# A graph-attention kernel: seven of eight key-tile pairs added before their row sums, six sum tiles, sums three steps behind

## The chip, the cores and the metric

The kernel runs on one NeuronCore of a Trainium2 chip. The metric is device time in microseconds, the median of three runs: 4205.73 us for the kernel before (4204.49 to 4206.44). Engines are named as the profile names them: PE is the matrix engine (PEld its weight load), DVE the vector engine, ACT the scalar engine, POOL the GpSimd engine, SP the engine that issues most DMAs.

## The reference, cut to what matters

Eight batches of 2048 nodes with 256 features go through two attention layers with four heads each, over one adjacency matrix. The change touches the second layer only:

```python
def _L1_gnn_ref(h, adj, W, a):
    ...
    q = (h @ W).reshape(B, N, H, D)
    a_src, a_dst = (a[:D], a[D:])
    e_src = jnp.einsum('bnhd,d->bnh', q, a_src)
    e_dst = jnp.einsum('bnhd,d->bnh', q, a_dst)
    e = e_src[:, :, None, :] + e_dst[:, None, :, :]
    e = jnp.where(e >= 0, e, ALPHA * e)
    mask = (adj > 0)[None, :, :, None]
    e = jnp.where(mask, e, NEG_INF)
    attn = jax.nn.softmax(e, axis=2)
    h_prime = jnp.einsum('bijh,bjhd->bihd', attn, q)
    return jax.nn.elu(h_prime.reshape(B, N, H * D))
```

The softmax needs two things for each node i: the weighted sum over the nodes j, and the plain sum of the weights over j, which divides it.

## The kernel before, in words

The first layer's loop (lines 748 to 788) is untouched. The second layer is one loop over 512 rounds (lines 901 to 952): 32 passes k (one batch and head each, `passes`), each of 16 steps jt, one for each tile of 128 key nodes j. The weights of a tile stand as 128 keys by 2048 queries, in four blocks of 512.

In a step, these things are issued:

- DVE makes the tile of weights e (`clipped`, L804) from near, which lies in PSUM and is written once a pass by ACT (`nears`, L795), from a number of its own for each key (far), and from the mask (limit). It does so two steps ahead of the rest (`ready`). There are five e tiles (`second_e`). At steps 0 and 15 the operation is split into two halves.
- PE multiplies the tile with the values (`weigh_rows`, L815), eight calls into two PSUM banks (acc).
- The sum over the keys is made on PE as well (`add_up_rows`, L826), four calls of the tile against for_sums into one PSUM bank (den). To spare such calls, two neighbouring tiles 2m and 2m+1, the pair m, are first brought together in t: at the even step ACT scales the first tile by the ratio of the two keys' factors into t (L926, two halves), at the odd step POOL adds the second tile to t (L932, two halves), and PE sums t LAG = 2 steps later, from the list `due`. Pairs 3 and 7 (`SINGLE`) are not added: PE sums each of their tiles unadded, in the step in which it comes. t has four buffers of 128 x 1024, so two pairs; they use memory (tag q) that the first layer needed for its queries.
- At step 15 ACT copies acc (cT, L939), PE makes the sums that are due, and ACT copies den (dT, L948). The pass's `ending` (lines 838 to 878) is then a generator that later steps carry on: PE transposes dT and cT, DVE makes the inverse and z (L848, L858), ACT four small operations for each half (L870 to L873), POOL two adds for each half (L875, L876), SP stores. Step 0 of the next pass begins with ACT's for_sums (L911).

`advance()`, at the end of every step but 13, moves such generators on: the ending, and during heads 0 to 2 the `preparation` of the next batch (normalised rows h, transposed hT, the values qn on PE and DVE, small work on POOL). Each engine carries out what it was given strictly in the order of issue, which is the order of this loop: a schedule written out by hand.

In the first passes the first layer's last block is still being finished (`finish`, L517 and L553 on POOL, tile o with two buffers); its last store of o falls into pass 1.

Of the kernel before, what the change touches and what calls it, by code (L numbers as in the profile page):

```python
# [27 lines left out]
def bcast(ap, axis, n):  # L28

    ap = ap.unsqueeze(axis)  # L30
    shape = list(ap.shape)
    shape[axis] = n
    return ap.broadcast_to(shape)
# [18 lines left out]
def layers(  # L52
# [24 lines left out]
    NQB = N // QB  # L77
    NKT = N // P
# [20 lines left out]
    def banks(name):  # L99
        return [psum.tile([P, QB], F32, tag=f"both{k}", name=name) for k in range(2)]  # L100
# [5 lines left out]
    def heads_tile(name, tag, bufs=2):  # L106
        return big.tile([P, 2, QB], F32, tag=tag, name=name, bufs=bufs)
# [105 lines left out]
    def advance(all_of=True, mask_first=False):  # L213

        moved = all_of and tick()
        for steps_of in sorted(aside, key=lambda steps_of: mask_first and steps_of is not all_limits):
            got = next(steps_of, aside)
            if got is aside:
                aside.remove(steps_of)
            moved = moved or got is not False  # L220
            if got is None:
                if here[0] < 0:
                    aside.append(aside.pop(aside.index(steps_of)))
                break
        return moved

    def drain(until=lambda: False):
        while not until() and advance():
            pass
# [359 lines left out]
    def sources(held, h, **place):  # L589

        es = []
        for half in range(2):
            e = big.tile([P, HALF], F32, name="es", **place)
            nc.sync.dma_start(
                e,
                held[h, 2 * half : 2 * half + 2, :, :]
                .rearrange("b c p -> (b c p)")
                .partition_broadcast(P),
            )
            es.append(e)  # L600
        return es
# [208 lines left out]
    def weigh_rows(jt, h, e, qn, acc):  # L810

        for part in range(2):
            own = slice(h * DH + 32 * part, h * DH + 32 * part + 32)
            for blk in range(NQB):
                nc.tensor.matmul(  # L815
                    acc[part][32 * blk : 32 * blk + 32, :],
                    qn[jt // NT][:, jt % NT, own],
                    e[:, blk, :],
                    start=(jt == 0),
                    stop=(jt == NKT - 1),  # L820
                )

    def add_up_rows(jt, blocks, for_sums, den, first, last):

        for blk in range(NQB):
            nc.tensor.matmul(  # L826
                den[32 * blk : 32 * blk + 32, :],
                for_sums[:, jt, :],
                blocks[blk],
                start=first,  # L830
                stop=last,
            )
# [44 lines left out]
            yield True  # L877
        nc.sync.dma_start(column(out[b], h), xs)

    LAG = 2  # L880
    SINGLE = (3, NKT // 2 - 1)
    first_layer.close()
    second_e = ctx.enter_context(tc.tile_pool(name="second_e", bufs=5))
    psum = ctx.enter_context(tc.tile_pool(name="second_psum", bufs=1, space=PSUM))
# [6 lines left out]
    def begun(k, jt):  # L891

        b, h = passes[k]
        if jt == 0:
            nears(near, following.pop(k), h, shared[b][2])
        return clipped(jt, h, near, shared[b][3], jt in (0, NKT - 1))
# [3 lines left out]
    due, ts, acc, den, before = [], None, None, None, None  # L900
    for s, (k, jt) in enumerate(rounds):
        here[0] = len(steps) + s // 4
        b, h = passes[k]
        qn, held, off_s, far, quot, share = shared[b]
        if s + 2 < len(rounds):
            ready.append(begun(*rounds[s + 2]))
        now = ready.pop(0)
        if jt == 0:
            acc = banks("acc1")
            for_sums = big.tile([P, NKT, 32], F32, tag="sr"[k % 2], name="for_sums", bufs=1)  # L910
            nc.scalar.copy(for_sums, bcast(share[:, :, h], 2, 32))  # L911
            if h == 0 and b + 1 < B:
                aside.append(preparation(b + 1))
        if jt == (2 if k % 4 < 3 else 8) and k + 1 < len(passes):
            b1, h1 = passes[k + 1]
            drain(lambda: b1 in shared)
            following[k + 1] = sources(shared[b1][1], h1, tag="add")
        weigh_rows(jt, h, now, qn, acc)
        m = jt // 2
        if m in SINGLE:  # L920
            due.append((s, jt, [now[:, blk, :] for blk in range(NQB)]))
        elif jt % 2 == 0:
            ts = []
            for half in range(2):
                t = heads_tile("t", "q", 4)
                nc.scalar.activation(  # L926
                    t, now[:, 2 * half : 2 * half + 2, :], AF.Copy, scale=quot[:, m, h : h + 1]
                )
                ts.append(t)
        else:  # L930
            for half in range(2):
                nc.gpsimd.tensor_tensor(  # L932
                    ts[half], ts[half], now[:, 2 * half : 2 * half + 2, :], ALU.add
                )
            due.append((s + LAG, jt, [ts[blk // 2][:, blk % 2, :] for blk in range(NQB)]))
        if jt == NKT - 1:
            cT = big.tile([P, 2, QB], F32, tag="hT", name="cT", bufs=1)
            for part in range(2):
                nc.scalar.copy(cT[:, part, :], acc[part])  # L939
        for entry in [entry for entry in due if entry[0] <= s]:  # L940
            due.remove(entry)
            _, j, blocks = entry
            if j == 1:
                den = rest[0][:, 0, :]
            add_up_rows(j, blocks, for_sums, den, j == 1, j == NKT - 1)
        if jt == NKT - 1:
            dT = const.tile([P, QB], F32, tag="wk", name="dT")
            nc.scalar.copy(dT, den)  # L948
            aside.insert(0, ending(k, cT, dT))

        if jt != NKT - 3:
            advance()
# [252 lines left out]
@with_exitstack  # L1205
def adj_preln_kernel(
    ctx: ExitStack,
    tc: tile.TileContext,
    x, adj, Wq, bq, Wk, bk, Wv, bv, Wo, bo, gamma, beta, W, a, out,
):  # L1210
    nc = tc.nc
    B, N, F = x.shape
    const = ctx.enter_context(tc.tile_pool(name="const", bufs=1))
    dram = ctx.enter_context(tc.tile_pool(name="dram", bufs=1, space=bass.MemoryType.DRAM))
    ident = const.tile([P, P], F32, tag="ident", name="ident")
    make_identity(nc, ident)
    x1 = [dram.tile([N, F], F32, tag=f"x1_{b}", name=f"x1_{b}") for b in range(B)]
    verdict = const.tile([1, 1], I32, tag="verdict", name="verdict")
    layers(
        tc, x, adj, Wq, bq, Wk, bk, Wv, bv, Wo, bo, gamma, beta, W, a, x1, out, ident, dram, verdict  # L1220
    )
    with tc.If(nc.values_load(verdict, min_val=0, max_val=1) != 0):  # L1222
        gat_layer(tc, x1, adj, W, a, out, ident)
# [35 lines left out]
```

## Time and profile before

| | us |
|---|---|
| median of three runs | 4205.73 |
| the profiled execution | 4210.55 |
| its span, first to last instruction | 4208.7 |
| second layer, first e tile to the last dT | 2729.1 to 4191.2 |
| mean granted clock of PE | 0.994 |

The profile comes from one execution. The page gives, for each engine, the busy time over the span; the windows view gives the same for a stretch; the timeline lists instructions in order, with the start, the duration (of several merged ones, if it says x2 or more: PE's matmuls count two records for a call), and in brackets the idle time of the engine before it and what ended it. The busiest groups of the second layer, from the page:

| line, engine | what | count | busy us | mean ns |
|---|---|---|---|---|
| L804 DVE | e (both widths) | 576 | 1183.0 | 2107 |
| L815 PE | acc | 8192 | 972.8 | 595 |
| L932 POOL | t + e | 384 | 903.9 | 2383 |
| L926 ACT | t from e | 384 | 420.1 | 1144 |
| L826 PE | sums of t | 1536 | 211.0 | 594 |
| L826 PE | sums of e | 1024 | 141.0 | 592 |

PE's records overlap, since several matmuls run side by side, so their mean is not the time that PE gives to one of them; the distance of their starts in the timeline is.

### The profile page before, as it was taken

The numbers are of one execution on the slowest core, as the hardware profiler recorded it, in microseconds if no ns is written. First come the engines' busy times: TensorE is split into PE (matmuls) and PEld (weight loads), VectorE is DVE, ScalarE is ACT, GpSimd is POOL, SyncE is SP. The second block draws the span as 40 slices with busy tenths as digits, with TensorE's granted clock in tenths as the row PEclk, the third lists the DMA queues.
The fourth block names the chain that finished last, engine by engine and source line by source line (L and its number), as shares of the span: only waits on it lengthen the run. The fifth ranks groups of instructions, "written<-read, shape, count | busy, mean of one in ns | idle before, by whom it ended". The sixth has DMA issues, their size and how long they took to land. (4 is left out here: it accounts for less than half of the span.)

```text
span 4208.7 us, 85702 instructions
## 1 busy us (share of the span) xinstructions
PE 4067.2 (97%) x34998; PEld 1507.0 (36%) x34998; DVE 3159.1 (75%) x3526; ACT 2394.9 (57%) x3090; POOL 3263.0 (78%) x1735
## 2 busy tenths in 40 slices
PE   7999999999999999999999999889999999999998
PEld 3333333333333333333333333333333333333333
DVE  5786676666766677676677677588888988888897
ACT  5655565555565565555556556564555646555554
POOL 2577787888888888788788799777776877777687
PEclk9999999999999999999999999999999999999999
DMA  3221211112112112111211222221221222122121
GB/s 112 87 77 50 57 58 48 53 53 65 48 55 63 48 51 61 54 50 53 62 50 54 55 60 62 80 58 51 63 71 33 72 52 73 51 63 71 33 61 37
DMA packets 343235, 248.11 MB, mean 59 GB/s; under 512 B 225840, under 2 KB 293168, under 8 KB 342832
## 3 DMA queue, kind: packets, MB, share of 16 engines
q1 hardware_dynamic: 337648, 223.66, 19.6%
q0 software_dynamic: 5184, 18.88, 1.2%
q8 instruction: 277, 4.54, 0.4%
q14 instruction: 126, 1.03, 0.1%
HBM read 204.15 MB, written 36.18 MB: 57 GB/s over the span
## 5 line engine op out<-in xcount | busy, mean ns | idle before, releaser
L449 DVE SCALAR_TENSOR_TENSOR E<-big,limit 128x1024 f32<-128x1024 f32 x1024 | 1181.9, 1217 | 646.1 <-PE big L441 627.9
L742 POOL TENSOR_TENSOR add<-E 128x1024 f32<-128x1024 f32 x512 | 1203.7, 2374 | 496.1 <-PE both L461 472.7
L455 ACT ACTIVATE E<-E 128x1024 f32<-128x1024 f32 x1024 | 1055.7, 1057 | 687.8 <-DVE E L449 669.1
L804 DVE SCALAR_TENSOR_TENSOR e<-near,far,limit 128x2048 f32<-128x2048 f32 (+1 forms) x576 | 1183.0, 2107 | 94.3 <-issue 55.0
L932 POOL TENSOR_TENSOR t<-t,e 128x1024 f32<-128x1024 f32 x384 | 903.9, 2383 | 346.4 <-ACT t L926 196.0
L461 PE MATMUL both<-E,v 128*32 128x512 f32 x8192 | 993.9, 594 | 0.2
L815 PE MATMUL acc<-e,qn 128*32 128x512 f32 x8192 | 972.8, 595 | 5.3 <-DVE e L804 5.1
L441 PE MATMUL big<-qT,kT 64*128 64x512 f32 x4096 | 959.4, 606 | 14.6 <-DVE E L449 12.5
L441 PEld LDWEIGHTS big<-qT,kT 64*128 64x128 f32 x4096 | 366.2, 187 | 587.7 <-issue 419.8
L926 ACT ACTIVATE t<-e,quot 128x1024 f32<-128x1024 f32 x384 | 420.1, 1144 | 266.5 <-DVE e L804 153.1
L501 POOL TENSOR_TENSOR acc<-acc,c 128x1024 f32<-128x1024 f32 x224 | 531.2, 2371 | 4.6 <-DVE c L499 4.6
L461 PEld LDWEIGHTS both<-E,v 128*32 128x32 f32 x8192 | 294.3, 109 | 535.8 <-issue 396.7
L815 PEld LDWEIGHTS acc<-e,qn 128*32 128x32 f32 x8192 | 271.8, 110 | 496.0 <-issue 451.4
L499 DVE TENSOR_TENSOR c<-both,r 128x512 f32<-128x512 f32 x448 | 308.7, 690 | 42.3 <-PE both L461 10.6
L472 PE MATMUL big<-add,ones 128*32 128x512 f32 x2048 | 280.7, 601 | 13.9 <-POOL add L742 3.4
L826 PE MATMUL rest<-t,for_sums 128*32 128x512 f32 x1536 | 211.0, 594 | 22.2 <-DVE z L858 9.5
L479 ACT COPY s<-big 128x512 f32<-128x512 f32 x256 | 149.8, 585 | 71.1 <-PE big L472 70.8
L826 PE MATMUL rest<-e,for_sums 128*32 128x512 f32 x1024 | 141.0, 592 | 0.0
L145 ACT ACTIVATE h<-x,off,rstd 128x256 f32<-128x256 f32 x256 | 139.2, 593 | 0.0
L154 PE MATMUL rest<-w,hT 128*32 128x256 f32 x1952 | 122.1, 392 | 10.7 <-DVE qn L693 6.6
L795 ACT ACTIVATE near<-es,off_s 128x1024 f32<-128x1024 f32 x64 | 71.6, 1119 | 106.8 <-DVE e L804 95.8
L154 PE MATMUL big<-hT,wk 128*32 128x512 f32 x1024 | 124.2, 600 | 7.0 <-ACT hT L165 5.8
(133 smaller groups left out, 3031.3 us busy)
## 6 DMA issues: line engine op xcount, KB each, us to landing
r<-inv SPq DMA_DIRECT2D x1024, 64.0 KB
x<-in_x_dram SPq DMA_DIRECT2D x96, 512.0 KB
es<-er SPq DMA_DIRECT2D x64, 512.0 KB
adj_in<-in_adj_dram SPq DMA_DIRECT2D x32, 512.0 KB
x<-o POOLq DMA_DIRECT2D x32, 512.0 KB, 3.3
xh<-x SPq DMA_DIRECT2D x32, 512.0 KB
out_dram<-xh SPq DMA_DIRECT2D x32, 512.0 KB
x<-x SPq DMA_DIRECT2D x28, 512.0 KB
```

What stands on the lines that cost most here:

```text
L441: nc.tensor.matmul(ps[:, hh, :], ks[kt // NT][own, hp, (kt % NT) * P : (kt % NT + 1) * P], qs[qb][own, hp, :], start=True, stop=True,)
L449: nc.vector.scalar_tensor_tensor(e, ps, -0.5, bcast(limit[:, qb, kt, :], 1, 2), ALU.max, ALU.min)
L455: nc.scalar.activation(e, e, AF.Exp, scale=0.25 * EDGE)
L461: nc.tensor.matmul(both[part][32 * h : 32 * h + 32, :], vs[kt // NT][:, kt % NT, mine], es[h // 2][:, h % 2, :], start=first, stop=not first,)
L499: nc.vector.tensor_tensor(to[:, part, :], both[part], r, ALU.mult)
L501: nc.gpsimd.tensor_tensor(acc, acc, to, ALU.add)
L742: nc.gpsimd.tensor_tensor(both, tiles[0][hp], tiles[1][hp], ALU.add)
L804: nc.vector.scalar_tensor_tensor(e[:, of, :], near[:, of, :], far[:, jt, h : h + 1], limit[:, of, jt, :], ALU.max, ALU.min,)
L815: nc.tensor.matmul(acc[part][32 * blk : 32 * blk + 32, :], qn[jt // NT][:, jt % NT, own], e[:, blk, :], start=(jt == 0), stop=(jt == NKT - 1),
L826: nc.tensor.matmul(den[32 * blk : 32 * blk + 32, :], for_sums[:, jt, :], blocks[blk], start=first, stop=last,)
L926: nc.scalar.activation(t, now[:, 2 * half : 2 * half + 2, :], AF.Copy, scale=quot[:, m, h : h + 1])
L932: nc.gpsimd.tensor_tensor(ts[half], ts[half], now[:, 2 * half : 2 * half + 2, :], ALU.add)
```

## The change

Pair 3 is added like the others; only pair 7 is still summed tile by tile. The sums come three steps after the addition instead of two, but never later than step 15. t gets two more buffers: from pass 3 on, pairs 2 and 5 use the two buffers of o, which the first layer has left; in passes 0 to 2 all pairs share the four of tag q.

```diff
-    LAG = 2
-    SINGLE = (3, NKT // 2 - 1)
+    LAG = 3
+    SINGLE = NKT // 2 - 1
...
-        if m in SINGLE:
+        if m == SINGLE:
             due.append((s, jt, [now[:, blk, :] for blk in range(NQB)]))
         elif jt % 2 == 0:
             ts = []
             for half in range(2):
-                t = heads_tile("t", "q", 4)
+                t = heads_tile("t", "o", 2) if k > 2 and m % 3 == 2 else heads_tile("t", "q", 4)
...
-            due.append((s + LAG, jt, [ts[blk // 2][:, blk % 2, :] for blk in range(NQB)]))
+            due.append((min(s + LAG, s - jt + NKT - 1), jt, [ts[blk // 2][:, blk % 2, :] for blk in range(NQB)]))
```

## The prediction

> **What bounds the kernel now.** The page first: which engine is full, over the whole span.
>
> ```profile
> PE 4067.2 (97%) x34998; PEld 1507.0 (36%) x34998; DVE 3159.1 (75%) x3526; ACT 2394.9 (57%) x3090; POOL 3263.0 (78%) x1735
> ```
>
> The change touches only the second layer, whose 32 passes (one head of one batch each) run from 2729 us to the end. A pass ends when dT (L948), its finished column of sums, is copied. I read the times of those copies from the timeline of ACT and cut the windows view there. From batch 1 to 6 the pass lengths repeat within 0.1 us, so four rows of batch 3 (heads 0 to 3) and one of the last batch stand for nearly all. The columns are window, length, then busy time of PE, weight load, DVE, ACT and POOL.
>
> ```profile
> core 0: us, PE busy (x) PEld busy (x) DVE busy (x) ACT busy (x) POOL busy (x), PEclk, DMA share, GB/s
> 3294.90:3341.50 46.60, 44.01 (x396) 14.35 (x392) 41.68 (x25) 29.16 (x42) 36.95 (x20) 1.00 0.34 103
> 3341.50:3384.30 42.80, 42.11 (x400) 14.57 (x404) 36.62 (x24) 27.14 (x38) 33.26 (x16) 1.00 0.23 54
> 3384.30:3437.20 52.90, 51.54 (x576) 19.19 (x568) 44.91 (x34) 22.67 (x31) 33.83 (x19) 1.00 0.10 22
> 3437.20:3478.50 41.30, 40.37 (x382) 14.88 (x384) 36.29 (x23) 21.90 (x26) 33.33 (x16) 1.00 0.25 69
> 4069.90:4110.30 40.40, 39.08 (x350) 13.94 (x348) 37.97 (x23) 21.86 (x27) 33.29 (x16) 1.00 0.21 59
> ```
>
> PE is idle 0.7 to 2.6 us a pass: it sets the pace in heads 1 to 3. In the last batch DVE is just as full: 37.97 us plus the 2.39 us in which it waits for ACT's near (L795) make the 40.4. POOL has 7 to 10 us free (19 in head 2), so the question is where that free time lies. The timelines of PE, ACT and POOL at the turn into a last-batch pass, and through it:
>
> ```profile
> 4067.87 1.07 PE L826 MATMUL rest<-t,for_sums 128*32 128x512 f32 x8
> 4068.73 1.07 PE L826 MATMUL rest<-e,for_sums 128*32 128x512 f32 x8
> 4069.59 2.48 PE L815 MATMUL acc<-e,qn 128*32 128x512 f32 x16
> ```
>
> ```profile
> 4069.86 0.58 ACT L948 COPY dT<-rest 128x512 f32<-128x512 f32 x1 [1.13 <-PE rest L826]
> 4070.34 0.62 ACT L911 COPY for_sums<-share 128x512 f32<-128x512 f32 x1
> 4070.86 2.20 ACT L926 ACTIVATE t<-e,quot 128x1024 f32<-128x1024 f32 x2
> ```
>
> ```profile
> 4072.53 4.71 POOL L932 TENSOR_TENSOR t<-t,e 128x1024 f32<-128x1024 f32 x2 [6.30 <-DVE e L804]
> 4077.42 4.70 POOL L932 TENSOR_TENSOR t<-t,e 128x1024 f32<-128x1024 f32 x2 [0.17 <-DVE e L804]
> 4082.63 1.29 POOL L875 TENSOR_TENSOR z<-z,low 128x512 f32<-128x512 f32 x1 [0.51 <-ACT z L872]
> 4083.99 1.29 POOL L876 TENSOR_TENSOR xh<-xh,z 128x512 f32<-128x512 f32 x1
> 4085.24 4.73 POOL L932 TENSOR_TENSOR t<-t,e 128x1024 f32<-128x1024 f32 x2
> 4089.93 1.29 POOL L875 TENSOR_TENSOR z<-z,low 128x512 f32<-128x512 f32 x1
> 4091.30 1.29 POOL L876 TENSOR_TENSOR xh<-xh,z 128x512 f32<-128x512 f32 x1
> 4092.54 14.12 POOL L932 TENSOR_TENSOR t<-t,e 128x1024 f32<-128x1024 f32 x6
> ```
>
> POOL's free time is one piece, 6.30 us before a pass's first pair; after it POOL runs almost without a gap to the last add of pair 6 (4106.66). PE sums that pair at step 15, sums the unadded pair 7, ACT copies dT, then builds for_sums, then the first t, and only then can POOL add again. Today DVE's second e tile (4072.36) comes 0.4 us later than t, so the loop is nearly closed, but not the bound.
>
> **The change, part by part.**
>
> *Removed:* for pair 3, two sums of e (steps 6 and 7) become one sum of t. A sum is 4 calls (8 records) and holds PE 4068.73 - 4067.87 = 0.86 us: 0.86 a pass, 27.5 us over 32.
>
> *Added on ACT:* two scalings L926, 2.20 us a pair. ACT is idle 17 to 30 us a pass: nothing. They stand at step 6, where ACT's next work (z of the second half, hT copies) is not late; if it were, at most 2.2 us a pass.
>
> *Added on POOL:* two adds L932. In 4092.54 to 4106.66 three pairs follow each other at (14.12 - 4.73)/2 = 4.69 us. POOL's order of issue puts pair 3 after the second z/xh and right before pair 4. Pairs 4 to 6 are already back to back there, so all of it is pushed on, less whatever gap stood in front of pair 4.
>
> *Sums a step later, six t buffers:* a pair is summed at step +3 instead of +2, but the min() keeps pair 6 at step 15, as now. Where sums came too early (PE's weight loads waited 41.8 us for POOL's t in 51 waits) the later step helps; the third pair of t buffers takes ACT's 113.3 us of waiting for L826 away, which POOL's work will outlast. In passes 0 to 2 t keeps four buffers with the later sums; POOL has 20 us free in 0 and 2. I take nothing for these. No DMA is added, removed or moved past another on SP's or POOL's queue.
>
> *The wait this makes:* PE's sum of pair 6 must wait for POOL. Behind it in PE's queue stand the sum of pair 7 and the next pass; behind that ACT's dT, for_sums and t; behind those POOL itself. A pass is then three terms: a, from dT to POOL's first add; r, POOL's run to the end of pair 6; c, from there to the next dT. Closed, c is 4069.86 - 4067.87 = 1.99 plus a hop of 0.1 = 2.09 (now 2.6 to 4.5, because PE comes later than POOL). And a is 0.48 + 0.52 on ACT to the start of t, 1.14 for its first half and a hop of 0.1: 2.24, which the trace shows in head 3 (3437.22 to 3439.46).
>
> - Last batch: now 2.67 + 34.13 + 3.64 = 40.44. After: r gains 4.69 and loses the 0.51 wait for z (POOL now gets there later): 2.24 + 38.31 + 2.09 = 42.64, **+2.20**.
> - Head 3: now 2.24 + 35.48 + 3.61. After 2.24 + 40.17 + 2.09 = 44.50, **+3.17**. Its waits of 1.50 and 0.50 us (DVE's e behind the last qn, z) come after dT too and stay.
> - Head 1: now 4.55 + 35.39 + 2.83. POOL waits 1.98 us before pair 4, which pair 3 fills: 4.55 + 38.10 + 2.09 = 44.74, **+1.97**. Its long a holds the hT copy and two h that ACT has in its queue there.
> - Head 0: now 2.67 + 39.47 + 4.46. A gap of 1.70 is filled: 2.24 + 42.46 + 2.09 = 46.79, **+0.19**.
> - Head 2: POOL has gaps of 2.82 and 2.90 us before pairs 5 and 6 and is done 8 us before PE asks. PE keeps the pace: -0.86, and because PE now starts 1.5 us later against DVE, about half of its 1.2 us of waits for the inverse and z goes too: **-1.5**.
>
> Batches 1 to 6: 6 x (0.19 + 1.97 - 1.5 + 3.17) = +23.0. Batch 0: pass 0 is PE's (-0.9); pass 1, where POOL also finishes the first layer's last block and is busy 39.2 of 45.2 us, 3.17 + 39.47 + 4.69 + 2.09 = 49.4 against 45.25 (+4.1); pass 2 -1.5; pass 3, 2.24 + 38.60 + 2.09 = 42.93 against 39.78 (+3.15): +4.9 in all. Last batch: 4 x 2.20 = +8.8; what follows the last dT is as before. Sum **+36.7 us**: the span goes from 4208.7 to about 4245 us. The profiled execution took 4210.55, 4.8 above the median of 4205.73; the difference is put on the median: **4242 us**.
>
> *The e buffers.* Five e tiles, and POOL now also holds tile 7 until pair 3 is added. DVE's step 12 needs tile 7, step 14 needs tile 9. In a last-batch pass POOL would free tile 9 some 1 us after DVE wants it even if the loop above did not exist: DVE alone would make a pass about 41.6, +1.2. It lies inside the loop's +2.2, and costs on top only if DVE's delay reaches the next pass's second e, up to 1 us a pass.
>
> *Where the Trainium skill weighs.* By "Perfetto Trace Analysis", section "Optimizing Scalar/DVE Operations", GpSimd and VectorE share a read port of SBUF, so moving work between them may not help. If each added add stopped DVE for its length, that were 32 x 4.7 = 150 us more. The rows say otherwise: L804's 2048-wide form takes 2342 ns where POOL is idle and 2344 where POOL adds throughout (largest 2353), and L932 stays within 2346 to 2422. I take 0. By the same page's "Identifying the Most-Contended Engine", PE's matmul time is no good measure and POOL's occupancy is, which makes POOL (78%) the engine to relieve. By the page's reading the PE cut is worth 0; by the rows above, where PE idles 0.7 us in 42.8, it is worth 0.86 wherever POOL is not asked for more, which leaves head 2.
>
> **Rivals.**
>
> 1. *POOL's free 6.3 us swallow the pair, and PE's saving is kept* (faster). PE is short of time in 28 passes: 28 x 0.86 = 24 us less, 4182. For it: POOL is idle more than 4.69 us in every pass. Against: the gap lies behind the deadline. Pair 6 is ready only 1.65 us before PE asks in the last batch (0.86 in head 1, 1.64 in head 3, 2.5 in head 0); this is faster only where filled gaps plus that lead exceed 4.69 + 0.86, true in head 2 alone.
> 2. *Only DVE's e buffers bind, the loop hides* (little slower): +1.2 in heads 3 and last, 0 in heads 0 and 1, -1.5 in head 2: 11 x 1.2 - 7 x 1.5 + 4 = +7, about 4212. It needs a and c to overlap with POOL's run; ACT's and PE's orders of issue speak against it.
> 3. *The loop plus lost cover* (slower still): PE's sums of pairs 3 to 5 also stall, and DVE's late tiles push the next pass: +1 us in some 25 passes, about 4267.
> 4. *The change does not do what it says:* PE's order of issue shows 128 calls fewer and pair 3 among the sums of t. Under 1%.
>
> **How the numbers follow.** The loop 0.66 (4225 to 4260), rival 1 0.11, rival 2 0.12, rival 3 0.10, change without effect 0.01. Within 0.2% (about what a measurement of this kernel can tell from no change) is 4197 to 4214: half of rival 2 and the last, 0.06. Faster 0.11, slower 0.83. The range 4218 to 4262 holds the loop, the upper part of rival 2 and half of rival 3; its low end is heads 1 and 3 gaining 1 us each back.
>
> **What would show it.** Right: passes of 42.6 in the last batch, 44.5 in heads 1 and 3, 46.8 in head 0, 51.4 in head 2; POOL's free piece shrunk to 4.3 us and ended by ACT's t, not by DVE's e; PE's sum of pair 6 starting 0.1 us after POOL's last add, PE idle 3 us before it; L804 and L932 at unchanged lengths. Wrong: PE reaching the sum of pair 6 after POOL (rival 1), POOL's first add still released by DVE (rival 2), L804 longer beside POOL (the port).

## The result, and the profile after

The changed kernel takes 4233.72 us (median of five runs; the kernel before took 4204.49 in the same job): 1.0070 times as long, 95% interval 1.0054 to 1.0086. That is +29.2 us; forecast were +36.7 and 4242 us. One of the five ran at a granted clock of 0.579, took 6665.06 us, and is left out of the ratio. The profiled execution took 4233.72, its span is 4231.9. First the page, then the windows view cut at the dT copies, for the same five passes as before (batch 3, heads 0 to 3, and one of the last batch); columns as above.

```profile
PE 4078.6 (96%) x34742; PEld 1495.5 (35%) x34742; DVE 3162.0 (75%) x3526; ACT 2463.1 (58%) x3154; POOL 3412.2 (81%) x1799
```

```profile
core 0: us, PE busy (x) PEld busy (x) DVE busy (x) ACT busy (x) POOL busy (x), PEclk, DMA share, GB/s
3302.60:3348.80 46.20, 43.78 (x385) 14.16 (x376) 38.26 (x23) 31.45 (x44) 41.49 (x22) 1.00 0.31 89
3348.80:3393.40 44.60, 42.83 (x396) 15.77 (x400) 39.58 (x25) 29.25 (x40) 37.88 (x18) 1.00 0.24 53
3393.40:3444.00 50.60, 50.37 (x564) 18.83 (x556) 43.62 (x34) 24.66 (x34) 38.48 (x21) 1.00 0.10 23
3444.00:3488.30 44.30, 42.30 (x380) 14.07 (x384) 38.44 (x24) 24.03 (x28) 37.97 (x18) 1.00 0.28 76
4088.00:4130.30 42.30, 40.29 (x344) 12.94 (x340) 38.21 (x23) 23.94 (x28) 37.89 (x18) 1.00 0.19 52
```

POOL has 4.6 us more in every pass. Heads 1 and 3 and the last batch are longer, head 2 is 2.4 us shorter and now PE's alone (50.37 of 50.60). In head 3 and the last batch neither PE nor DVE is full any more (last batch: PE 40.29, DVE 38.21 of 42.30). The timelines of PE, ACT and POOL at the turn of a pass in the last batch show why:

```profile
4086.07 0.62 PE L826 MATMUL rest<-t,for_sums 128*32 128x512 f32 x2 [0.75 <-POOL t L932]
```

```profile
4088.03 0.59 ACT L948 COPY dT<-rest 128x512 f32<-128x512 f32 x1 [2.36 <-PE rest L826]
4088.51 0.62 ACT L911 COPY for_sums<-share 128x512 f32<-128x512 f32 x1
4089.03 4.28 ACT L926 ACTIVATE t<-e,quot 128x1024 f32<-128x1024 f32 x4
```

```profile
4083.65 2.37 POOL L932 TENSOR_TENSOR t<-t,e 128x1024 f32<-128x1024 f32 x1
4090.26 9.43 POOL L932 TENSOR_TENSOR t<-t,e 128x1024 f32<-128x1024 f32 x4 [4.24 <-ACT t L926]
...
4109.58 18.74 POOL L932 TENSOR_TENSOR t<-t,e 128x1024 f32<-128x1024 f32 x8
4132.56 2.39 POOL L932 TENSOR_TENSOR t<-t,e 128x1024 f32<-128x1024 f32 x1 [4.24 <-ACT t L926]
```

Read in order of time it is one ring. POOL's last add of pair 6 ends at 4086.02; PE's sum of its second half starts 0.05 us later; dT follows at 4088.03, for_sums, t, and POOL adds again at 4090.26, released by ACT's t where DVE's e released it before. POOL's free piece is 4.24 us (it was 6.30), and each of its two ends is now set by POOL itself. The next free piece begins 4.24 us before 4132.56: a period of 42.30.

Pass lengths below are distances of the dT copies. The first layer is not touched, and its end moves between 2722.3 and 2729.1 us from profile to profile, so I compare the sum of the 32 passes instead of spans. Heads are medians of batches 1 to 6.

| kernel | head 0 | head 1 | head 2 | head 3 | last batch | 32 passes against before | median, us |
|---|---|---|---|---|---|---|---|
| before | 46.62 | 42.77 | 52.91 | 41.33 | 40.44 | 0 | 4204.5 |
| changed | 46.23 | 44.61 | 50.55 | 44.35 | 42.27 | +29.5 | 4233.7 |
| no adds of pair 3 | 44.64 | 42.76 | 50.59 | 41.51 | 40.43 | -22.6 | 4182.9 |
| half of the adds of pair 3 | 44.12 | 42.74 | 50.60 | 42.02 | 40.43 | -16.8 | 4186.0 |
| deferred | 45.67 | 41.91 | 53.52 | 40.08 | 41.37 | +2.0 | 4207.2 |
| add only | 47.78 | 45.09 | 51.75 | 44.82 | 42.73 | +50.5 | 4255.9 |
| sums later, six buffers | 44.16 | 43.06 | 52.31 | 41.51 | 40.43 | -15.8 | 4188.5 |
| sums later only | 44.16 | 43.06 | 52.31 | 41.52 | 40.43 | -14.5 | 4190.4 |
| six buffers only | 46.62 | 42.77 | 52.91 | 41.34 | 40.43 | +0.1 | 4203.3 |
| pair 3 added in head 2 only | 44.16 | 43.06 | 51.45 | 41.52 | 40.43 | -18.9 | 4184.7 |

### The profile page after: what moved, and what is told of

Its sections match the earlier page's. It is cut to its first block, busy times and chain, and to the rows that moved or that the text cites. A ratio compares the mean times of both kernels' runs of the same rounds, so it can differ in the third digit from the quotient of the medians.

```text
span 4231.9 us, 85391 instructions
## 1 busy us (share of the span) xinstructions
PE 4078.6 (96%) x34742; PEld 1495.5 (35%) x34742; DVE 3162.0 (75%) x3526; ACT 2463.1 (58%) x3154; POOL 3412.2 (81%) x1799
## 5 line engine op out<-in xcount | busy, mean ns | idle before, releaser
L804 DVE SCALAR_TENSOR_TENSOR e<-near,far,limit 128x2048 f32<-128x2048 f32 (+1 forms) x576 | 1186.6, 2105 | 141.4 <-POOL t L932 118.0
L932 POOL TENSOR_TENSOR t<-t,e 128x1024 f32<-128x1024 f32 x448 | 1053.2, 2388 | 235.2 <-ACT t L926 205.5
L815 PE MATMUL acc<-e,qn 128*32 128x512 f32 x8192 | 1008.0, 596 | 8.7 <-DVE e L804 8.0
L926 ACT ACTIVATE t<-e,quot 128x1024 f32<-128x1024 f32 x448 | 488.3, 1142 | 197.1 <-DVE e L804 129.0
L826 PE MATMUL rest<-t,for_sums 128*32 128x512 f32 x1792 | 293.7, 595 | 33.1 <-POOL t L932 30.1
L826 PEld LDWEIGHTS rest<-t,for_sums 128*32 128x32 f32 x1792 | 67.2, 109 | 212.7 <-issue 113.1
```

The costliest lines, as they stand in the source:

```text
L804: nc.vector.scalar_tensor_tensor(e[:, of, :], near[:, of, :], far[:, jt, h : h + 1], limit[:, of, jt, :], ALU.max, ALU.min,)
L815: nc.tensor.matmul(acc[part][32 * blk : 32 * blk + 32, :], qn[jt // NT][:, jt % NT, own], e[:, blk, :], start=(jt == 0), stop=(jt == NKT - 1),
L826: nc.tensor.matmul(den[32 * blk : 32 * blk + 32, :], for_sums[:, jt, :], blocks[blk], start=first, stop=last,)
L926: nc.scalar.activation(t, now[:, 2 * half : 2 * half + 2, :], AF.Copy, scale=quot[:, m, h : h + 1])
L932: nc.gpsimd.tensor_tensor(ts[half], ts[half], now[:, 2 * half : 2 * half + 2, :], ALU.add)
```

## The experiments

The theory is the ring: POOL's adds, PE's sum of pair 6, dT, for_sums, t, POOL. Its rivals are a cost of POOL's adds by their sheer time (port, or an engine that is full), and a cost of the later sums. Ratios are to the kernel before in the same job: 4206.39 us for the runs without the adds, deferred, addition alone and rest alone, 4204.25 for the other four. Differences in us between runs of different jobs carry the 2 us by which the jobs differ. The diffs shown are against the changed kernel. The runs with none or half of pair 3's adds leave tile 7, or half of it, out of the row sums.

**Without the adds of pair 3.**

```diff
-            for half in range(2):
+            for half in range(2) if m != 3 else ():
                 nc.gpsimd.tensor_tensor(
```

> Pair 3 is scaled and summed as one tile, but POOL's two adds for it are left out, so tile 7 is missing from the row sums. Theory (the loop through POOL's 4.69 us of added work): POOL's run is back to six pairs, PE keeps its 0.86 us, so the passes of the last batch return to about 40.4 us, head 1 to about 41.9, head 3 to about 40.5, head 2 stays near 50.5: about 4180 us (4172 to 4190). Rival (the loss lies in the longer PE order, the later sums or the added ACT work, not in POOL's adds): it stays above 4220 us.

Measured: 4182.86 us, 0.9940 (0.9927 to 0.9954), as expected, though heads 1 and 3 took 0.9 and 1.0 us more than expected. By the sums of the passes, two POOL instructions a pass are worth 52 us over 32 passes, although POOL is idle 4.4 us a pass even with them in the last batch. The loss is theirs: ACT's scaling and the new order of PE's sums are still in this run.

**The sum of pair 6 and dT one step later.** The ring is cut in the order of issue; nothing of the work changes.

```diff
-            due.append((min(s + LAG, s - jt + NKT - 1), jt, [...]))
+            due.append((s + LAG, jt, [...], k, for_sums))
...
-            add_up_rows(j, blocks, for_sums, den, j == 1, j == NKT - 1)
-        if jt == NKT - 1:
-            dT = const.tile([P, QB], F32, tag="wk", name="dT")
-            nc.scalar.copy(dT, den)
-            aside.insert(0, ending(k, cT, dT))
+            add_up_rows(j, blocks, sums_of, den, j == 1, j == NKT - 3)
+            if j == NKT - 3:
+                column_done(of, cT, den)
...
```

(column_done holds the three lines taken out; after the last round the same is done for what is left in `due`.)

> All seven pairs are added as in the changed kernel, but the sum of pair 6 and the copy dT that follows it move to step 0 of the next pass (no min() any more), so the next pass's for_sums and t no longer stand behind them in ACT's queue. Theory (a closed loop POOL, PE's last sum, dT, for_sums, t, POOL): the loop opens, POOL's first add starts with DVE's second e again, and the next bounds are the five e tiles in the last batch and head 3 (about 41.6 us a pass) and PE elsewhere: about 4193 us (4185 to 4210). Rival (POOL simply has too much to do): no change, above 4225 us.

Measured: 4207.20 us, 1.0003 (0.9995 to 1.0012), inside the expected range but 14 us above its centre. With the same POOL work the passes lose 2.0 us instead of 29.5. ACT's and POOL's timelines at the turn (here L917 is for_sums, L932 ACT's t, L904 dT, L938 POOL's add):

```profile
4063.50 0.62 ACT L917 COPY for_sums<-share 128x512 f32<-128x512 f32 x1
4064.02 2.19 ACT L932 ACTIVATE t<-e,quot 128x1024 f32<-128x1024 f32 x2
4067.12 0.59 ACT L904 COPY dT<-rest 128x512 f32<-128x512 f32 x1 [0.90 <-PE rest L826]
```

```profile
4059.24 4.73 POOL L938 TENSOR_TENSOR t<-t,e 128x1024 f32<-128x1024 f32 x2
4066.67 9.39 POOL L938 TENSOR_TENSOR t<-t,e 128x1024 f32<-128x1024 f32 x4 [2.69 <-DVE e L804]
```

The t of the next pass now stands ahead of dT, and POOL is again released by DVE's e. A last-batch pass takes 41.37 us, not 40.44: DVE waits 0.85 us for POOL's hold on an e tile, which is the e-buffer bound (41.6 in the prediction):

```profile
4096.01 4.73 DVE L804 SCALAR_TENSOR_TENSOR e<-near,far,limit 128x2048 f32<-128x2048 f32 x3 [0.85 <-POOL t L938]
```

Passes 0 and 1 are 5 and 6 us longer than in the kernel before. Head 2 is 3.0 us longer than in the changed kernel, head 3 4.3 shorter. I did not trace either to its instruction.

**Half of the adds of pair 3.**

```diff
-            for half in range(2):
+            for half in range(1 if m == 3 else 2):
                 nc.gpsimd.tensor_tensor(
```

> As the changed kernel, but POOL adds only the first half of pair 3, so the row sums lack tile 7 for half of the queries. Theory (a loop through POOL that has to grow past the other bounds before it costs anything): 2.36 us less than the changed kernel brings the last batch from 42.3 back to DVE's 40.4, head 3 to about 42.0, head 1 to PE's and DVE's 42.8, head 0 to about 44.6: about 4188 us (4182 to 4197), nearly all of the way back to the kernel without the adds. Rival (POOL's adds cost by their sheer time, through a port or through the engine's total): half of the way, about 4208 us.

Measured: 4185.96 us, 0.9957 (0.9944 to 0.9971). With no add 4182.9, with one 4186.0, with two 4233.7: the first costs 3 us, the second 48. By the sums of the passes it is 5.8 and 46.3, and all of the 5.8 lies in batch 0; in batches 1 to 6 and the last the first half costs nothing. That is a ring growing past other bounds, not a price by the microsecond of POOL.

**The addition alone**, with sums two steps behind and four buffers (`LAG = 2`, all t of tag q).

> Pair 3 is added, but the sums stay two steps behind and t keeps four buffers. Theory: the loop is as closed as in the changed kernel, since pair 6 is summed at step 15 in both; on top of it t waits for the sums of four buffers: 4233 to 4255 us. Rival (the addition is harmless, the later sums cost): about 4205 us or less.

Measured: 4255.89 us, 1.0116 (1.0100 to 1.0131), 0.9 us above the theory's range and far from the rival's. So the rest of the change does not cost but gives: 22 us (21 by the sums of the passes).

**The rest of the change alone**, pairs 3 and 7 unadded.

```diff
-    SINGLE = NKT // 2 - 1
+    SINGLE = (3, NKT // 2 - 1)
...
-        if m == SINGLE:
+        if m in SINGLE:
```

> Pairs 3 and 7 stay unadded as in the kernel before; only the sums come three steps behind and t has six buffers. Theory: POOL has no more work than before, so no loss; the later sums take a few of PE's waits away: about 4200 us (4192 to 4206). Rival (the later sums make the loss, because they push PE's sums toward the end of the pass): above 4220 us.

Measured: 4188.49 us, 0.9957 (0.9943 to 0.9970): a gain larger than either expectation allowed. To see which half makes it, two more runs. **Sums three steps behind, four buffers:**

> Pairs 3 and 7 unadded, sums three steps behind, but t keeps its four buffers. Theory: t then has to wait for a sum that is issued in the same step, so the gain of the run with six buffers is mostly lost: about 4206 us (4198 to 4212). Rival (the later sums alone make that gain): about 4188 us.

Measured: 4190.38 us, 0.9966 (0.9954 to 0.9978). My theory was wrong here, the rival right. **Six buffers, sums two steps behind:**

> Pairs 3 and 7 unadded, six buffers of t, but sums two steps behind as before. Theory: PE's sums still stand where the waits for the ending's z and for POOL's t are: about 4203 us (4198 to 4207). Rival (ACT's waits for t buffers were the cost): about 4188 us.

Measured: 4203.31 us, 0.9997 (0.9989 to 1.0005). The buffers give nothing that can be seen; the later sums are the gain. The waits of PE in the kernel before name it (who waited for whom, us in total, times, longest):

```profile
PE rest L826 <- DVE z L858: 9.5, 24, 0.4
PE rest L826 <- POOL t L932: 9.4, 8, 1.3
```

In the run with later sums and four buffers the first row is gone, and the second is

```profile
PE rest L826 <- POOL t L932: 0.2, 1, 0.2
```

A sum issued one step later meets an ended z and a finished t. The two rows add to 18.9 us, where 14.5 to 15.8 us of pass time went. Nearly all of the gain is in head 0 (46.62 to 44.16; head 2 gains 0.6, heads 1 and 3 lose 0.3 and 0.2). There PE stood, in the kernel before, for a pair that POOL had only just added, with the next batch's transposes behind it:

```profile
3318.50 0.62 PE L826 MATMUL rest<-t,for_sums 128*32 128x512 f32 x2 [1.25 <-POOL t L932]
```

With 0.44 for z the two rows are 1.7 of the 2.46 us of this pass; the rest I did not trace. In the changed kernel the second row is back, larger, at pair 3 and at the deadline:

```profile
PE rest L826 <- POOL t L932: 30.1, 37, 1.4
```

The six buffers are a place where a rule of the Trainium skill is to be weighed: "Perfetto Trace Analysis", section "Optimization Strategy", says that the same gap repeating, on the engine that should be saturated, can mean too few buffers. ACT, busy 57% of the span, is not that engine. Two more buffers took its 113.3 us of waiting for t buffers down to 8.8, its waiting for DVE's e rose from 153.1 to 209.4, and the time changed by -0.03%. With later sums and four buffers ACT's wait for buffers was 206.0 us, and the kernel was faster.

**Pair 3 added where POOL has room**, an attempt at a faster kernel.

```diff
-        if m == SINGLE:
+        if m == SINGLE or m == 3 and (k < 3 or h != 2 or b == B - 1):
```

> Later sums and six buffers; pair 3 is added only in head 2 of batches 1 to 6, where POOL has gaps, and stays unadded elsewhere. Theory: head 2 takes 50.6 us as in the changed kernel instead of 52.3, the other passes stay as with unadded pairs: 4188.5 - 6 x 1.7 = about 4178 us (4173 to 4184). Rival (head 2's gain was only possible because the passes before it had been slowed): about 4188 us.

Measured: 4184.69 us, 0.9953 (0.9939 to 0.9967), between the two expectations and 0.7 us above the theory's range. It is the fastest complete kernel here by its times (4183.94 to 4185.88; in the same job, later sums with four buffers took 4186.87 to 4194.03). Its pass sum is 3 us below that of later sums with six buffers, but that run stood in the other job, and by the ratios (0.9953 and 0.9957) the two are not told apart. Head 2 went to 51.45, by 0.86 and no more: one sum of PE. The other 0.86 that head 2 gains in the changed kernel seems to need head 1's sum to be gone as well, so that PE enters head 2 ahead (in the run without the adds head 1 takes 42.76 and head 2 50.59). That last step is read from the table, not tried by itself.

## Why the prediction was right, point by point

The direction, the mechanism and most sizes held: the ring with its three terms a, r and c. Measured for the last batch: a 2.23, r 38.03, c 2.01, against 2.24, 38.31, 2.09.

| pass | forecast | measured | what differed |
|---|---|---|---|
| head 0 | +0.19 | -0.39 | waits of 0.16 and 0.18 before pairs 1 and 6 also filled |
| head 1 | +1.97 | +1.84 | r 38.05 against 38.10, c 2.01 against 2.09 |
| head 2 | -1.5 | -2.36 | nearly all of PE's waits went, not half |
| head 3 | +3.17 | +3.02 | c and r smaller by 0.1 each |
| last batch | +2.20 | +1.83 | r smaller by 0.28: another 0.17 wait filled |
| pass 0 | -0.9 | +2.51 | see below |
| pass 1 | +4.1 | +4.10 | |
| pass 2 | -1.5 | -0.39 | see below |
| pass 3 | +3.15 | +3.01 | |

- *PE's saving of 27.5 us.* Rightly not counted where POOL closes the ring, but over-valued elsewhere. "It sets the pace in heads 1 to 3" holds in head 2 only: without the adds of pair 3, one sum less leaves head 1 at 42.76 (43.06 with it) and head 3 at 41.51 in both. The runs without the add and with unadded pairs differ by 6.8 us of pass time for the 27.5 of PE (pass 0 alone loses 3.0 there). So the first rival's 24 us were not to be had in that way. That PE idles less than 1 us of 41 in head 3 did not make it the bound; what bounds head 3 there was not tested.
- *"Sums a step later, six t buffers: I take nothing for these."* This is the term that was mis-sized: -15 us alone, and -21 us in the changed kernel against the addition alone. Where the ring sets the length of a pass, the predicted c of 2.09 already rests on the later sums, without saying so. The last batch of the addition alone, then of the changed kernel:

```profile
4130.26 18.72 POOL L932 TENSOR_TENSOR t<-t,e 128x1024 f32<-128x1024 f32 x8
4148.68 0.60 PE L826 MATMUL rest<-t,for_sums 128*32 128x512 f32 x2
```

```profile
4126.57 0.60 PE L826 MATMUL rest<-t,for_sums 128*32 128x512 f32 x2
4128.37 0.62 PE L826 MATMUL rest<-t,for_sums 128*32 128x512 f32 x2 [0.77 <-POOL t L932]
```

With sums two steps behind, PE waits for POOL at five earlier places of this pass (2.7 us), starts the sum of pair 6 only 0.3 us before POOL ends (4148.97), and c is 2.48. With later sums it starts 1.75 us before POOL's end (4128.32), waits 0.77, and c is 2.01. So the stalls of rival 3 are real: PE waits 61.5 us in all for POOL's t in the addition alone (+50.5 us), and 30.1 in the changed kernel. In heads 0 and 2 the forecast was 0.6 and 0.9 us a pass too high; later sums alone gain 2.5 and 0.6 there. The row to read was PE's own wait, 18.9 us; I read the weight loads' 41.8 and took nothing for it.
- *The same sentence for passes 0 to 2.* There the later sums meet only four buffers. Pass 0 takes 62.14 in the changed kernel and 62.13 also without POOL's adds of pair 3, but 58.70 with the adds and sums two steps behind, and 59.2 to 60.8 in three runs with later sums and pair 3 unadded. So it takes both the later sums and the t of pair 3: ACT's t waits for a sum, with h behind it in its queue, which PE's transposes need.

```profile
2768.40 2.19 ACT L926 ACTIVATE t<-e,quot 128x1024 f32<-128x1024 f32 x2 [2.33 <-PE rest L826]
2770.50 1.08 ACT L145 ACTIVATE h<-x,off,rstd 128x256 f32<-128x256 f32 x2
```

```profile
2771.14 0.93 PE L157 MATMUL rest<-ident,h 128*128 128x128 f32 x4 [1.11 <-ACT h L145]
```

PE's waits for h in pass 0 are 4.6 us, against 1.8 in the kernel before. "POOL has 20 us free" was no answer to that. (With half of the adds pass 0 took 65.34; these lengths scatter by more than those of the later passes. Pass 2 I did not trace: with later sums and pair 3 unadded it takes 54.3 us, 0.4 more than before.)
- *Luck.* Part of the nearness of the total is luck: pass 0, forecast 3.4 us too short, cancels head 0, forecast 0.6 us too long six times.
- *c.* The predicted "PE idle 3 us before the sum" was wrong as a sign: PE waits 0.77 there, since it sums the first half while POOL adds the second, and has waited 1.03 before the second half of pair 3.
- *The port.* Taken at 0, and L804 stays at 1272 to 2353 ns while POOL adds a sixth more; L932, 2346 to 2422 ns before, takes 2338 to 2436.
- *The e buffers*, +1.2 a pass if the ring were gone: +0.9 in the deferred run.

## What to carry to other kernels

Free time of an engine is worth only what comes before its deadline: follow its last result through the in-order queues behind it, and if the chain comes back to the engine, add the terms of that ring. Such a ring is cheap until it is the longest (3 us for the first half of the work, 48 for the second), and can be cut by the order of issue alone. And when a change bundles parts, size the one that "costs nothing" too: here a sum moved by one step gained 14 to 18 us, and in the changed kernel hid two fifths of what the addition lost.

## What the runs showed of the hardware

Nothing that was not expected: POOL's 128x1024 f32 adds run at the same 2.34 to 2.44 us, and DVE's e tiles at the same length, with 384 or 448 adds. The granted clock was 0.995 in the changed kernel and 0.994 before.
